# First four pairs of a two-by-two block product: eight products a group, or seven a group with the two groups in turn

## The chip, the cores and the metric

The kernel runs on one core of one Trainium2 chip. The core has a matrix engine (TensorE, PE in the tables; the loading of its stationary operand is PEld), a vector engine (VectorE, DVE), a scalar engine (ScalarE, ACT), a general engine (GpSimd, POOL) and a queue that mostly starts transfers (SyncE, SP). Each engine takes its instructions strictly in the order written for it, and waits where an operand is not ready or a buffer is not free. The metric is device time of one execution in microseconds; lower is better. A difference of 0.2% is about what a measurement of this kernel can tell.

## The reference

`x` is 64 batches of 64 x 1024 numbers. Cut to what matters:

```python
W = weights[condition]                    # per batch a 64 x 64 matrix, one of 16
c = einsum('bct,bcd->bdt', x, W)          # mixes the 64 rows of a batch
logits = c @ gate_w.T + expert_bias       # 4 experts
top1 = argmax(logits)
base = c @ W_up.T                         # 1024 x 1024
z = c @ lora_A.T                          # 4 experts x rank 8
out = x + base + (z of the top expert) @ lora_B of that expert
```

The kernel uses that the mixing of rows and the product over columns can be exchanged: it first forms `u = x @ w` with `w` = gate, lora_A and W_up side by side (1024 x 1060), and then mixes the rows of `u` by a block-diagonal matrix of two batches.

## The kernel before

**Tiling.** A *pair* is two batches: 128 rows of 1024 numbers. There are 32 pairs, and a *group* `g` is the pairs `a = 2g` and `b = 2g + 1`. The product of a group is a two-by-two block product. On the left A11 and A12 are the two column halves of pair a, A21 and A22 those of pair b (each 128 x 512, loaded transposed by `load_half`, L102). On the right B11, B12, B21, B22 are the quarters of `w`, 512 x 530 each: the first index is the half of the 1024 rows, the second the half of the 1060 columns. A block of `w` is handled in four slices k of 128 rows.

**Precision.** Each operand is kept as a high part (rounded to the format in which the matrix engine multiplies) and a low part (the remainder). ACT writes the high part, DVE then subtracts it from the original: `split_a` (L131) for the left, `split_b` (L148) and `split_bs` (L158) for the right. Every product is three matrix products (high-high, high-low, low-high) for each of 4 slices and 2 column banks: 24 matmuls of 264 or 266 columns (`part_of_product`, L198).

**Groups 0 and 1** (`eight`, L505) form all eight block products. In group 0, two products share each of B11 and B21 (a *double* step: for each k first the one pair and then the other); the rest are single. `h` and `at(s, k, ...)` are a table written out by hand: after slice k of step s (k = -1: ahead of the step) the listed work is put into the queues. `run` (L491) and `product` (L214) write out matmuls and hooks in that order, and the wrapper `InOrder` (L35) holds PE, DVE, ACT, POOL and most of SP to it.

**Groups 2 to 15** (`seven`, L622) form seven products each from sums of blocks: S1 to S4 on the left (`sums`, L109) and T1 to T4 on the right. The T blocks are built once, while groups 0 and 1 run: `sum_t1` (L169) subtracts B12 from B11, and `add_to` (L165) starts a transfer on POOL that adds another block of `w` to a tile in place. B11 and B12 are loaded a second time for it (`load_two`, L154). B12 was split for groups 0 and 1 into the memory that T4 takes later.

**After a product** the sums in PSUM become `u` (`u_of` L255, `u_sum` L262: high part by ACT, low part by DVE). For each of three column ranges of a pair, `apply` (L312) mixes the rows, `gate` (L322) picks the expert (six small DVE instructions), `turn` (L341) transposes the result on PE and splits it (ACT, then DVE), `delta` (L349) adds the expert's part, and `evict` (L355) copies to `y` on ACT. After the third range POOL starts a transfer that adds `x` to `y`, and when it has landed SP stores `y`.

PSUM holds three accumulators (`chain`, L195). Work tiles of 530 columns come from a pool of ten (`temp`, L98), halves of `x` from a pool of six, split left operands from a pool of four.

## Time and profile before

| | |
|---|---|
| median of 3 runs | 414.96 us (414.76 to 415.2) |
| the profiled execution: its own time | 415.4 us |
| its span, first to last instruction | 413.6 us |
| busy: PE, DVE, ACT, POOL | 408.5, 285.6, 185.0, 75.0 us |
| granted TensorE clock, mean | 0.999 |
| first matmul of the products | 4.20 us |
| end of the first double step | 12.16 us |
| first matmul of group 2 | about 57.7 us |
| one group of seven afterwards | 24.79 us for two groups (75.40 to 100.19 in the chain) |

The span is 1.8 us shorter than the execution's own time, and that execution is 0.4 us above the median. A busy share is a mean over all stages: DVE has 69% over the span, but 44.64 of the first 57.75 us (77%). The time of a matmul in the groups (about 287 ns) is its own from start to end; in a stream the next starts about 0.124 us after it, since they are pipelined.

### The profile page before, as it was taken

Reading aid. Unit: us, or ns where it says so; the run is one execution under the profiler, and the core shown is the slowest. Engines: PE = TensorE matmul, PEld = TensorE weight load, DVE = VectorE, ACT = ScalarE, POOL = GpSimd, SP = SyncE. Lnnn points to the kernel's source line nnn. Section 1 sums busy time; section 2 is a strip of 40 time slices with the busy share of each in tenths; the row PEclk is TensorE's granted clock in tenths of the full one; section 3 lists DMA queues with packets and bytes.
Section 4 is the critical chain, followed back from the end, with each engine's and each line's share of the span. In section 5 each row is a group of like instructions: output and inputs, shape, how many; then the busy total and the mean of one; then the engine's idle time right before and its main releaser. Section 6 shows DMA issues by size and latency. Waiting matters only on the chain.

```text
span 413.6 us, 8160 instructions
## 1 busy us (share of the span) xinstructions
PE 408.5 (99%) x3191; PEld 407.7 (99%) x3191; DVE 285.6 (69%) x648; ACT 185.0 (45%) x419; POOL 75.0 (18%) x92
## 2 busy tenths in 40 slices
PE   8999999999999999999999999999999999999996
PEld 8999999999999999999999999999999999999995
DVE  5987776876767666676676767666676676766766
ACT  5846734453534445333343534445333344533531
POOL 4304502020020202102020020202102020020000
PEclk9999999999999999999999999999999999999999
DMA  8889964553556435465453555434465443564345
GB/s 276 301 305 224 241 167 98 137 123 99 172 133 177 92 93 143 124 178 135 103 127 98 164 135 159 128 81 138 122 179 135 104 126 94 169 165 124 52 101 178
DMA packets 25830, 60.99 MB, mean 147 GB/s; under 512 B 3328, under 2 KB 5344, under 8 KB 25792
## 3 DMA queue, kind: packets, MB, share of 16 engines
q1 hardware_dynamic: 18112, 40.48, 27.2%
q0 software_dynamic: 6704, 19.21, 27.1%
q10 hardware_dynamic: 976, 0.79, 0.6%
q8 instruction: 25, 0.41, 0.4%
q14 instruction: 13, 0.11, 0.1%
HBM read 43.68 MB, written 16.78 MB: 146 GB/s over the span
## 4 chain that ended last, share of the span: by engine, by line
PE 97%; DMA 1%; issue 0%; POOL 0%; DVE 0%; POOLq 0%
PE c L43 81%; PE o L43 16%; DMA cond_sb<-in_cond_dram 1%; DVE y L43 0%; POOL which L43 0%; POOL condf L43 0%; POOLq L43 0%; POOLq L818 0%
## 5 line engine op out<-in xcount | busy, mean ns | idle before, releaser
L43 PE MATMUL c<-hT,ah 128*128 128x264 f32 x480 | 139.7, 291 | 0.0
L43 PE MATMUL c<-lT,ah 128*128 128x264 f32 x480 | 137.3, 286 | 0.0
L43 PE MATMUL c<-hT,al 128*128 128x264 f32 x480 | 137.1, 286 | 0.0
L43 PE MATMUL c<-hB,ah 128*128 128x264 f32 (+1 forms) x424 | 121.8, 289 | 0.0
L43 PE MATMUL c<-hB,al 128*128 128x264 f32 (+1 forms) x424 | 121.0, 287 | 0.0
L43 PE MATMUL c<-lB,ah 128*128 128x264 f32 (+1 forms) x424 | 119.0, 287 | 0.0
L43 PEld LDWEIGHTS c<-lT,ah 128*128 128x128 f32 x480 | 91.0, 190 | 0.0
L43 PEld LDWEIGHTS c<-hT,ah 128*128 128x128 f32 x480 | 90.9, 189 | 0.0
L43 PEld LDWEIGHTS c<-hT,al 128*128 128x128 f32 x480 | 90.6, 189 | 0.0
L43 POOL DMA_DIRECT2D y<-in_x_dram x31 | 29.3, 945 | 290.3 <-ACT y L43 285.3
L43 PEld LDWEIGHTS c<-hB,ah 128*128 128x128 f32 x424 | 80.7, 190 | 0.3 <-ACT hB L43 0.2
L43 PEld LDWEIGHTS c<-hB,al 128*128 128x128 f32 x424 | 80.7, 190 | 0.0
L43 PEld LDWEIGHTS c<-lB,ah 128*128 128x128 f32 x424 | 79.5, 190 | 0.2 <-issue 0.2
L43 ACT COPY y<-o 128x352 f32<-128x352 f32 (+1 forms) x91 | 40.1, 443 | 58.4 <-PE o L43 55.0
L43 ACT CAST uh<-usum 128x530 fp32r<-128x530 f32 (+4 forms) x44 | 27.1, 616 | 68.4 <-DVE usum L43 68.4
L43 DVE TENSOR_TENSOR al<-S,ah 128x512 fp32r<-128x512 f32 x56 | 38.5, 688 | 24.2 <-ACT ah L43 24.2
L43 DVE TENSOR_TENSOR al<-xh,ah 128x512 fp32r<-128x512 f32 x46 | 31.7, 689 | 30.0 <-ACT ah L43 30.0
L43 PE MATMUL o<-uh,bd 128*128 128x356 f32 (+2 forms) x186 | 44.7, 322 | 0.0
L43 DVE TENSOR_TENSOR ul<-usum,uh 128x530 fp32r<-128x530 f32 (+4 forms) x44 | 30.0, 682 | 18.6 <-ACT uh L43 18.6
L43 ACT CAST zt<-o 96x128 fp32r<-96x128 f32 x31 | 8.1, 262 | 76.0 <-PE o L43 76.0
L43 POOL DMA_INDIRECT wsel<-in_cw_dram,idx x32 | 34.9, 1089 | 10.6 <-issue 5.2
L43 ACT CAST ah<-S 128x512 fp32r<-128x512 f32 x56 | 34.9, 623 | 1.8 <-DVE S L43 1.4
(88 smaller groups left out, 471.3 us busy)
## 6 DMA issues: line engine op xcount, KB each, us to landing
xh<-in_xt_dram SPq DMA_DIRECT2D x60, 256.0 KB
y<-in_x_dram POOLq DMA_DIRECT2D x30, 512.0 KB, 5.6
out_dram<-y SPq DMA_DIRECT2D x30, 512.0 KB
wraw<-in_w_dram SPq DMA_DIRECT2D x23, 265.0 KB
T<-in_w_dram POOLq DMA_DIRECT2D x8, 265.0 KB, 7.3
xx<-in_xt_dram SPq DMA_DIRECT2D x1, 512.0 KB
wsel<-in_cw_dram,idx POOLq DMA_INDIRECT x32, 5.0
y<-in_x_dram SPq DMA_DIRECT2D x1, 512.0 KB
```

Source lines behind the costliest of these rows:

```text
L43: return lambda *a, **k: self.tc.keep_in_program_order(fn(*a, **k))
```

## The change

Groups 0 and 1 are run together by one function, `front`, in place of `eight(0)` and `eight(1)`, with seven products for each: first both groups' A11 by B11 and A12 by B21 as double steps (the first taken pairs are 0 and 2, where they were 0 and 1), then S4 by B22, S1 by T1, S2 by T2, S3 by T3 and A22 by T4, each for group 0 and then for group 1: 14 products instead of 16. B12 is neither loaded nor split. T1 is the plain copy of B11, negated in place, with B12 added by a transfer (two slices in one); T2 is T1 minus B22, computed on DVE; T3 is the negated B22 with B12 added; T4 is T2's tile with B21 added. The plain copies of B11 and B22 stay in memory that the low and high parts of T3 take later. The signs of S1 to S4 and T1 to T4 change accordingly.

In PSUM, `p` holds A11 B11 and then A11 B11 + A12 B21; `q` is S4 B22; `s` collects S1 T1, S2 T2, S3 T3 and A22 T4 one after another. What is needed of a state in between is copied out: A11 B11 alone (`keep_p`, ACT), it plus q (`add_p`, DVE) and it minus S1 T1 (`less_s`, DVE). In the second double step the products of group 0 for k = 0 and 1 are put ahead of those of group 1, with the work listed for k = 0 and k = 1 after each of them.

The diff, cut to its core:

```diff
-    wh["B12"], wl["B12"] = wh["T4"], wl["T4"]
+    before = {
+        q: cpool.tile([P, KH if q != "T2" else 2, NB], F32, name=q, tag=tag)
+        for q, tag in (("B11", "lT3"), ("B22", "hT3"), ("T3", "hT4"), ("T2", "lT4b"))
+    }
...
-        (sync if i < 4 else nc.sync).dma_start(t, xt[i, hf])
+        (sync if i < 6 else nc.sync).dma_start(t, xt[i, hf])
...
+            "S1": (vector.tensor_add, (b, 0), (b, 1)),
+            "S2": (vector.tensor_sub, (a, 0), (g, "S1")),
+            "S3": (vector.tensor_sub, (b, 0), (a, 0)),
+            "S4": (vector.tensor_add, (a, 1), (g, "S2")),
...
+    def start_t1(s):
+        t = before["B11"][:, s]
+        scalar.mul(t, t, -1.0)
+        add_block("T1", s, "B12")
+    def start_t3(s):
+        scalar.mul(before["T3"][:, s], before["B22"][:, s], -1.0)
+        add_block("T3", s, "B12")
+    def end_t1(s):
+        high_t("T1", s)
+        for ks, t in pieces_of("T2", s):
+            vector.tensor_sub(t, before["B11"][:, ks], before["B22"][:, ks])
+        low_t("T1", s)
+    def end_t2(s):
+        high_t("T2", s)
+        low_t("T2", s)
+        add_block("T2", s, "B21")
...
-                raw[i, hf] = t[:, i]
+                raw[2 * i, hf] = t[:, i]
...
+    for i in (1, 3):
+        for hf in range(2):
+            load_half(i, hf)
+    for k in range(KH):
+        load_b("B22", k)
...
+        at(0, 0, split_b, "B21", 0)
+        at(0, 1, split_b, "B21", 1)
+        at(0, 1, split_a, 1, "A12")
+        at(0, 2, split_b, "B21", 2)
+        at(0, 3, split_b, "B21", 3)
+        at(1, -1, load_b3)
+        at(1, -1, keep_p, 0)
+        at(1, -1, keep_p, 1)
+        for m in ("S1", "S2", "S4"):
+            at(1, 0, sums, 0, m)
+        at(1, 0, split_a, 0, "S4")
+        at(1, 1, start_t1, TWOS[0])
+        at(1, 1, split_b, "B22", 0)
+        for m in ("S1", "S2", "S4"):
+            at(1, 1, sums, 1, m)
+        at(1, 2, start_t1, TWOS[1])
+        at(1, 2, split_b, "B22", 1)
+        at(1, 2, split_a, 1, "S4")
+        at(1, 3, split_cond, 0)
+        at(2, -1, lambda: u_of(0, 0, c["p", 0]))
+        at(2, 0, split_b, "B22", 2)
+        at(2, 0, lambda: u_of(2, 0, c["p", 1]))
+        at(2, 1, split_b, "B22", 3)
+        at(2, 2, split_a, 0, "S1")
+        at(2, 3, split_b3, PARTS[0])
+        at(2, 3, apply, 0, 0)
+        at(2, 3, gate, 0)
+        at(3, -1, add_p, 0)
+        at(3, 0, end_t1, TWOS[0])
+        at(3, 1, split_a, 1, "S1")
+        at(3, 2, end_t1, TWOS[1])
+        for s in TWOS:
+            at(3, 3, start_t3, s)
+        at(3, 3, turn, 0)
+        at(3, 3, split_cond, 2)
+        at(4, -1, add_p, 1)
+        at(4, 0, end_t2, TWOS[0])
+        at(4, 1, delta, 0, 0)
+        at(4, 1, evict, 0, 0)
+        at(4, 1, split_b3, PARTS[1])
+        at(4, 1, apply, 2, 0)
+        at(4, 1, gate, 2)
+        at(4, 2, split_a, 0, "S2")
+        at(4, 3, end_t2, TWOS[1])
+        at(5, -1, less_s, 0)
+        at(5, 1, turn, 2)
+        at(5, 1, split_a, 1, "S2")
+        at(5, 2, sums, 0, "S3")
+        at(5, 3, delta, 2, 0)
+        at(5, 3, evict, 2, 0)
+        at(6, -1, less_s, 1)
+        at(6, 0, split_a, 0, "S3")
+        at(6, 1, end_t3, TWOS[0])
+        at(6, 1, sums, 1, "S3")
+        at(6, 2, load_half, 5, 0)
+        at(6, 2, load_half, 5, 1)
+        at(6, 3, end_t3, TWOS[1])
+        at(7, -1, lambda: u_sum(0, 1, c["s", 0], ts["q", 0]))
+        at(7, 0, split_a, 1, "S3")
+        at(7, 2, finish, 0, 1)
+        at(7, 3, finish, 0, 2)
+        at(8, -1, lambda: u_sum(2, 1, c["s", 1], ts["q", 1]))
+        at(8, 0, split_a, 0, "A22")
+        at(8, 1, end_t4, TWOS[0])
+        at(8, 2, finish, 2, 1)
+        at(8, 3, finish, 2, 2)
+        at(8, 3, load_half, 4, 0)
+        at(8, 3, load_half, 4, 1)
+        at(8, 3, split_a, 1, "A22")
+        at(9, -1, lambda: u_sum(1, 1, c["s", 0], ts["p", 0]))
+        at(9, 0, end_t4, TWOS[1])
+        at(9, 1, sums, 2, "S1")
+        at(9, 2, split_cond, 1)
+        at(9, 2, split_cond, 3)
...
+        at(10, -1, lambda: u_sum(3, 1, c["s", 1], ts["p", 1]))
+        at(10, 0, sums, 2, "S2")
+        at(10, 1, split_a, 2, "A11")
+        at(10, 2, sums, 2, "S3")
+        at(11, -1, lambda: u_sum(1, 0, c["s", 0], ts["r", 0]))
+        at(11, 0, split_a, 2, "S2")
+        at(11, 1, sums, 2, "S4")
...
-            at(0, 0, lambda: u_of(pb, 0, cp["1"]))
+            at(0, 0, lambda: u_sum(pb, 0, cp["s", 1], ts["r", 1]))
...
-            for k in range(KH):
-                at(1 + k, 3, split_b, "T4", k)
```

## The prediction

> **What bounds the kernel now.** First the page's busy times and the chain that ended last:

> ```profile
> PE 408.5 (99%) x3191; PEld 407.7 (99%) x3191; DVE 285.6 (69%) x648; ACT 185.0 (45%) x419; POOL 75.0 (18%) x92
> PE c L43 81%; PE o L43 16%; DMA cond_sb<-in_cond_dram 1%; DVE y L43 0%; POOL which L43 0%; POOL condf L43 0%; POOLq L43 0%; POOLq L818 0%
> ```

> PE carries 97% of the chain. The chain in order of time gives the price of a product:

> ```profile
> 7.43 13.04 PE c L43 x102
> 66.45 2.97 PE c L43 x24
> ```

> 24 matmuls take 2.97 us, 0.124 us each. PE waits for nobody after 7.43 us. So a matmul less is worth its time only while the other engines stay ahead. How far ahead are they in the changed stage? Busy time by stretch (columns: length, then PE, PEld, DVE, ACT, POOL, clock, DMA share, GB/s):

> ```profile
> 0.00:12.20 12.20, 11.05 (x81) 10.61 (x82) 6.81 (x21) 7.43 (x17) 6.53 (x23) 1.00 0.86 295
> 0.00:57.75 57.75, 56.60 (x443) 56.16 (x444) 44.64 (x93) 35.72 (x74) 19.82 (x37) 1.00 0.93 268
> 15.00:20.00 5.00, 5.00 (x43) 5.00 (x42) 4.84 (x11) 4.56 (x11) 0.00 (x0) 1.00 0.78 248
> ```

> Group 2 begins at 57.75. Until then DVE works 44.64 us; ahead of 12.2 us it is idle for 12.2 - 6.8 = 5.4 us, waiting for loads, and from 15 to 20 us it is full. Not PE but DVE is short here.

> **Durations**, from the rows in order of time:

> ```profile
> 11.96 1.71 ACT L43 CAST hB<-wraw 128x530 fp32r<-128x530 f32 x3
> 18.19 0.59 ACT L43 CAST uh<-c 128x530 fp32r<-128x530 f32 x1
> 18.68 0.64 ACT L43 CAST hB<-wraw 128x530 fp32r<-128x530 f32 x1
> 12.80 1.94 DVE L43 TENSOR_TENSOR lB<-wraw,hB 128x530 fp32r<-128x530 f32 x3
> 52.44 0.97 DVE L43 TENSOR_TENSOR bd<-wsel,bd 64x64 fp32r<-64x64 f32 x4
> 21.00 0.16 DVE L43 TENSOR_TENSOR lg<-o,bias_sb 128x4 f32<-128x4 f32 x1 [0.71 <-PE o L43]
> 22.40 0.70 DVE L43 TENSOR_TENSOR ul<-c,uh 128x530 fp32r<-128x530 f32 x1
> ```

> From start to start ACT takes 0.54 us for 530 columns, 0.49 from PSUM (18.19 to 18.68). DVE takes 0.62 for 530, 0.60 for 512 (sums and splits follow one another at that step from 54.65 us), 0.25 for a 64 x 64 piece, 1.40 for the six of a gate (21.00 to 22.40). Two slices in one (1060 columns) are not in the trace: no more than two singles (1.24 DVE, 1.08 ACT) and no less than two without the second one's fixed part (264 columns start every 0.35 and 0.32 us, so 1.16 and 0.98). I take 1.16 and 0.98, the rows' slope.

> **What goes and comes, by amount.** PE loses 2 x 24 matmuls: 48 x 0.124 = 5.9 us. The mixing, turning and expert matmuls stay the same in number. On DVE, until group 2: gone are 4 lows of B12, 8 subtractions for T1 and T3 and 12 lows of T1 to T3, 24 x 0.62 = 14.9. In come T1 to T4 as 7 wide and 6 single ones (7 x 1.16 + 6 x 0.62 = 11.9), 8 sums S (4.8), 14 left splits for 8 (3.6), 4 of `add_p` and `less_s` (2.5) and 5 sums ahead of `u` (3.1). Net 25.9 - 14.9 = +11.0. DVE then has 44.6 + 11.0 + 5.4 idle at the start = 61.0 us ahead of group 2, without any other pause. PE's matmuls alone would be there at 57.75 - 5.9 = 51.8. This floor says +3.3 us, and the order of the queues decides what comes on top. Transfers: 12 plain loads of 265 KB less, adding transfers 3.25 MB for 2.1; POOL issues 7 for 8.

> **The queues, step by step** (the program order of the changed kernel, laid on the clock with these durations; the same done to the old program gives no wait of PE and its transpositions at 22.95 and 28.86 us, where the trace has 23.00 and 28.93).

> 1. *Second double step.* `keep_p` must copy A11 B11 out before PE may add to that accumulator. On ACT it stands behind all four B21 casts, the last of which ends at 13.67 (11.96 + 1.71). Copy 0.49 and hand-over 0.1: 14.25. PE is ready at 12.16. **2.1**. The matmuls queued behind all wait.
> 2. *S4 by B22, group 0*, from 14.25 + 5.94 = 20.2. DVE: three sums from 14.75 to 16.6; ACT split 17.2, then on ACT negation of B11 (0.98), B22 slice 0, negation, slice 1. DVE: low of S4 at 17.4, low of slice 0 to 19.5, then three sums of group 1 (21.3), slice 1 (21.95), low of S4 (22.6), two `bd` pieces, a `u` (23.8), slice 2 (24.4), a `u`, slice 3 (25.65). PE waits at slice 1 for 0.9, slice 2 for the cast 0.9 and the low 0.8, slice 3 for 0.5: **3.1**. End 26.3.
> 3. *S1 by T1.* S4 by B22 of group 1, apply and turn take PE to 29.9. DVE goes on: low of S1 26.2, b3 piece, gate after its apply 27.0 to 28.5, `add_p` 29.1, T2 half 30.3, low of T1 31.5. **1.6**. `delta` of pair 0 then waits for a turned z that stands behind split, two T2 slices and T1's second low: 34.75 for 32.9, **1.9**, and 0.2 for `bd`.
> 4. *Step 5*: the gate of pair 2 stands behind `add_p`, T2's low and the larger b3 piece, **0.8** at the turn, and its z behind split, two lows and `less_s`: **1.2**.
> 5. *S2 by T2 of group 1, `finish` of pair 0*: its `u` is summed after two T3 lows and two S3, at 48.4; cast 49.0, low 49.8. PE is there at 47.45: **1.7 and 0.4**.
> 6. *A22 by T4, group 1*: the accumulator is free when `u_sum` of pair 3 has read it, behind two T4 lows, S1 and four `bd` pieces: **1.3**.
> 7. *Into group 2.* The half of pair 4 is on SP in program order behind the stores of pairs 0 and 2, and the second store waits for the transfer that adds x. Rows for that:

> ```profile
> 35.12 0.86 POOL L43 DMA_DIRECT2D y<-in_x_dram  x1 [0.39 <-ACT y L43]
> 66.01 0.86 POOL L43 DMA_DIRECT2D y<-in_x_dram  x1 [13.81 <-ACT y L43]
> 43.63 6.99 SPq L374 DMA_DIRECT2D out_dram<-y  x2
> 71.18 0.34 SPq L374 DMA_DIRECT2D out_dram<-y  x1
> T<-in_w_dram POOLq DMA_DIRECT2D x8, 265.0 KB, 7.3
> ```

> The store follows its addition by 5.2 us in a quiet stage and 8.5 in the crowded front. Eviction ends at 56.5; the adding transfers for T are over by then, so I take 5.5: store 62.0, load 62.5. A load of 256 KB alone is not shown; the first ones (issued at 0.74, used from 3.4) say 2.6, behind a 512 KB store at up to 392 GB/s (the best stretch) 3.9: 65.1 to 66.4, taken 65.9, cast and low to 67.0 where PE is ready at 66.1. **0.9**. While DVE waits for that half in S2, the sum for `u` of pair 1 stands behind it: **1.4 and 0.4** at its apply, **0.3** at the turn, **2.0** at `delta` behind the `u` of pair 3 and a split.

> Sum of waits: 2.1 + 3.1 + 1.6 + 1.9 + 0.2 + 0.8 + 1.2 + 2.1 + 1.3 + 5.0 = 19.3. Less 5.9: +13.4. After that the groups run as before. The profiled execution would span 413.6 + 13.4 = 427.0 (415.4 + 13.4 = 428.8 with what lies around it); it stood 0.4 above the median, which gives 414.96 + 13.4 = **428.4 us**.

> Costed at nothing: T1's transfer, started at 18.3 and 20.1, landing 7.3 to 8.5 later (26.8, 28.6). It is hidden only because DVE comes to T2 at 29.1; with a faster DVE it would be the next to be late. T3 and T2 start at 30 to 41 and are used at 44 to 59.

> [...] The clock row reads 1.00 in every stretch up to 400 us, and 0.96 from 400 to 414 us where PE is busy for only 9.68 of 14. [...]

> **Rivals.**
> - *The cover holds* (faster): PE stays without a wait, 414.96 - 5.9 = 409.0. For it: no wait in 400 us, DVE idle for 31% of the span. Against: the 61.0 us floor. It decides where all waits together are below 5.9. 4%.
> - *Only steps 1 and 2 wait*: 414.96 - 5.9 + 5.2 = 414.3, no difference. It needs DVE to catch up from 26 us on, against the same floor. 3%.
> - *DVE catches up by step 5*, so that 5 to 7 (8.4) vanish: 420.0. For it: ACT and DVE have pauses after 43 us, waiting for each other and for PE. 16%.
> - *More*: additions land after 8.5 us as in the crowded front (3.0 more in step 7), or one clock window: 431.4, both 433. 19%.
> - My sum, 425 to 431 in itself: 58%.
> - That the 48 matmuls do not go is excluded: program order has them gone.

> The range, 419.5 to 432.5, takes in the catch-up and most of the last. Within 0.2% (0.83 us, about what a measurement tells from no change) lies only part of the second rival: 2%; faster 5%, slower 93%.

> **What would show it.** In the profile after: 3143 matmuls; the first long idle of PE at 12.2 us with ACT as releaser; DVE (lB, lT, zt) as releaser between 21 and 42; DVE near full from 13 to 50 us; group 2's first matmul at 66 to 67.5; from about 85 us the same 24.8 us for two groups. I am wrong if PE is past the second double step before 19 us, or if ACT has its copies ahead of the B21 casts.

## The result, and the profile after

The changed kernel takes 431.22 us (median of four, 430.84 to 433.02), the kernel before beside it 415.0 us: 1.0399 times, 95% interval 1.037 to 1.0429. That is slower by 16.2 us; 428.4 was predicted, with a range to 432.5.

First the page's busy times and the chain by engine, profile of the changed kernel:

```profile
PE 409.4 (95%) x3143; PEld 404.8 (94%) x3143; DVE 295.1 (69%) x657; ACT 187.9 (44%) x417; POOL 76.0 (18%) x91
PE 83%; DVE 8%; DMA 5%; ACT 2%; issue 1%; DVEq 0%; ACTq 0%
```

The 48 matmuls are gone (3143 for 3191), but PE carries only 83% of the chain, where it had 97%. The same stretches as before (length, PE, PEld, DVE, ACT, POOL, clock, DMA share, GB/s), and the fullest ones:

```profile
0.00:12.20 12.20, 10.51 (x80) 9.73 (x80) 7.63 (x22) 8.16 (x18) 7.35 (x24) 1.00 0.87 298
0.00:57.75 57.75, 48.21 (x334) 45.46 (x335) 45.79 (x87) 35.87 (x65) 17.82 (x34) 0.94 0.74 177
20.00:30.00 10.00, 8.62 (x63) 7.80 (x61) 9.18 (x20) 7.51 (x13) 0.70 (x1) 1.00 0.78 138
30.00:40.00 10.00, 6.99 (x40) 6.56 (x40) 9.64 (x20) 5.50 (x11) 3.55 (x3) 0.83 0.75 119
```

By 57.75 us PE has done 334 matmuls instead of 443, and DVE is at 92 and 96% from 20 to 40 us. The clock is no longer 1.00 (0.94 up to 57.75 us, 0.83 from 30 to 40). What PE waited for, from its rows in order of time (start, length, what; in brackets the idle time ahead and who ended it):

```profile
13.48 0.39 PE L43 MATMUL c<-hB,ah 128*128 128x264 f32 x1 [1.98 <-ACT t L43]
...
23.41 0.39 PE L43 MATMUL c<-hB,ah 128*128 128x264 f32 x1 [0.76 <-ACT hB L43]
...
31.32 0.39 PE L43 MATMUL c<-lT,ah 128*128 128x264 f32 x1 [1.31 <-DVE lT L43]
...
34.66 0.41 PE L43 MATMUL o<-b,zt 96*128 96x320 f32 x1 [1.70 <-DVE zt L43]
...
49.48 0.58 PE L43 MATMUL o<-uh,bd 128*128 128x352 f32 x2 [1.67 <-ACT uh L43]
...
63.81 0.39 PE L43 MATMUL c<-hT,ah 128*128 128x264 f32 x1 [1.22 <-DVE usum L43]
...
67.76 0.39 PE L43 MATMUL c<-hB,ah 128*128 128x264 f32 x1 [0.72 <-ACT ah L43]
...
70.38 0.60 PE L43 MATMUL o<-uh,bd 128*128 128x356 f32 x2 [1.12 <-ACT uh L43]
...
76.56 0.42 PE L43 MATMUL o<-b,zt 96*128 96x320 f32 x1 [1.87 <-DVE zt L43]
```

These are the places that the prediction named. From 80 to 400 us PE waits for nobody. The last addition to y is then done at 424.70 us, against 410.16 before: +14.5. The span is 15.5 longer; the last us lies behind that addition (4.4 us to the end for 3.4): the last transfer that adds `x` is issued 15.4 us later (419.69 for 404.33), and SP's last stores begin as much later (423.72 for 408.30). Why it is issued late was not looked into. Step 7's load, in the chain in order of time:

```profile
61.53 0.60 DVE S L43
...
62.87 4.20 DMA xh<-in_xt_dram
...
67.09 0.69 DVE S L43
```

One thing the prediction did not have. PE's stretches of 3.4 us (length, PE busy, clock, DMA share, GB/s):

```profile
11.20:14.60 3.40, 1.42 (x12) 1.00 1.06 377
14.60:18.00 3.40, 3.40 (x18) 0.52 1.09 355
...
31.60:35.00 3.40, 1.70 (x13) 1.00 0.77 115
35.00:38.40 3.40, 3.40 (x16) 0.53 1.11 197
```

After 3.4 us in which PE was busy for 1.42 or 1.70, it ran 3.4 us at half clock (0.52 and 0.53): 18 or 16 matmuls in a stretch that holds 27.

### The profile page after: what moved, and what is told of

Read it like the earlier page. It is cut to its first block, busy times and chain, and to the rows that moved or that the text cites. A ratio compares the mean times of both kernels' runs of the same rounds, so it can differ in the third digit from the quotient of the medians.

```text
span 429.1 us, 8033 instructions
## 1 busy us (share of the span) xinstructions
PE 409.4 (95%) x3143; PEld 404.8 (94%) x3143; DVE 295.1 (69%) x657; ACT 187.9 (44%) x417; POOL 76.0 (18%) x91
## 4 chain that ended last, share of the span: by engine, by line
PE 83%; DVE 8%; DMA 5%; ACT 2%; issue 1%; DVEq 0%; ACTq 0%
PE c L43 68%; PE o L43 15%; DMA xh<-in_xt_dram 2%; DMA xx<-in_xt_dram 2%; DVE lT L43 1%; DVE S L43 1%; DVE al L43 1%; DMA b3f<-in_lb_dram 1%; DVE ul L43 1%; ACT uh L43 1%; DVE usum L43 1%; DVE T L43 1%; ACT hT L43 0%; DVE t L43 0%; ACT ah L43 0%
## 5 line engine op out<-in xcount | busy, mean ns | idle before, releaser
L43 PE MATMUL c<-hT,ah 128*128 128x264 f32 (+1 forms) x512 | 149.4, 292 | 1.2 <-DVE usum L43 1.2
L43 PE MATMUL c<-hT,al 128*128 128x264 f32 (+1 forms) x512 | 146.5, 286 | 0.0
L43 PE MATMUL c<-hB,ah 128*128 128x264 f32 x376 | 108.9, 291 | 3.5 <-ACT t L43 2.0
L43 PE MATMUL c<-lT,ah 128*128 128x264 f32 (+1 forms) x384 | 110.1, 287 | 1.3 <-DVE lT L43 1.3
L43 PE MATMUL c<-hB,al 128*128 128x264 f32 x376 | 107.8, 288 | 0.2 <-DVE al L43 0.2
L43 PE MATMUL c<-lB,ah 128*128 128x264 f32 x376 | 106.1, 289 | 0.6 <-DVE lB L43 0.6
L43 PEld LDWEIGHTS c<-hT,ah 128*128 128x128 f32 x512 | 97.2, 190 | 1.4 <-DVE usum L43 1.4
L43 PEld LDWEIGHTS c<-hT,al 128*128 128x128 f32 x512 | 97.2, 190 | 0.0
L43 POOL DMA_DIRECT2D y<-in_x_dram x31 | 28.5, 918 | 309.9 <-ACT y L43 304.1
L43 PEld LDWEIGHTS c<-hB,ah 128*128 128x128 f32 x376 | 72.0, 191 | 4.2 <-ACT t L43 2.2
L43 PEld LDWEIGHTS c<-lT,ah 128*128 128x128 f32 x384 | 73.3, 191 | 1.5 <-DVE lT L43 1.5
L43 PEld LDWEIGHTS c<-lB,ah 128*128 128x128 f32 x376 | 71.1, 192 | 1.4 <-DVE lB L43 1.2
L43 PEld LDWEIGHTS c<-hB,al 128*128 128x128 f32 x376 | 71.8, 191 | 0.4 <-DVE al L43 0.4
L43 ACT COPY y<-o 128x352 f32<-128x352 f32 (+1 forms) x91 | 40.2, 442 | 64.0 <-PE o L43 62.0
L43 ACT CAST uh<-usum 128x530 fp32r<-128x530 f32 (+4 forms) x50 | 30.9, 618 | 80.1 <-DVE usum L43 80.1
L43 DVE TENSOR_TENSOR al<-S,ah 128x512 fp32r<-128x512 f32 x64 | 44.0, 688 | 26.2 <-ACT ah L43 26.1
L43 DVE TENSOR_TENSOR al<-xh,ah 128x512 fp32r<-128x512 f32 x44 | 30.4, 690 | 31.5 <-ACT ah L43 31.5
L43 DVE TENSOR_TENSOR ul<-usum,uh 128x530 fp32r<-128x530 f32 (+4 forms) x50 | 34.3, 685 | 23.1 <-ACT uh L43 23.1
L43 PE MATMUL o<-uh,bd 128*128 128x356 f32 (+2 forms) x186 | 45.7, 326 | 2.8 <-ACT uh L43 2.8
L43 ACT CAST ah<-S 128x512 fp32r<-128x512 f32 x64 | 39.9, 623 | 4.3 <-DVE S L43 3.9
L43 ACT CAST zt<-o 96x128 fp32r<-96x128 f32 x31 | 8.1, 260 | 76.3 <-PE o L43 76.3
L43 POOL DMA_INDIRECT wsel<-in_cw_dram,idx x32 | 35.7, 1114 | 11.4 <-issue 4.9
## 6 DMA issues: line engine op xcount, KB each, us to landing
B<-in_w_dram SPq DMA_DIRECT2D x7, 265.0 KB, 6.0
wraw<-in_w_dram SPq DMA_DIRECT2D x4, 265.0 KB, 6.0
T<-in_w_dram POOLq DMA_DIRECT2D x2, 265.0 KB, 5.1
```

The source lines that it names most:

```text
L43: return lambda *a, **k: self.tc.keep_in_program_order(fn(*a, **k))
```

## The experiments

Two explanations had to be told apart, and a third came with the trace: the order of ACT's and DVE's queues (the prediction), single prices that add up however they stand, and the clock. All kernels start from the changed one. Times in us; "over before" is each median less that of before measured beside it; half clock and PE's idle time (waits over 0.15, from 10 to 80-100 us) are of the profiled execution, which is one of the two (e7) to four behind each median. Beside the different runs before lies between 414.46 and 415.0 us, so two of them are compared by the time over before. The half clock leaves out the first microseconds, ahead of the trace's first entry of the clock (at 4.5 us in the changed kernel; more on this in the last section).

| run | edit | median | over before | half clock | PE idle |
|---|---|---|---|---|---|
| changed kernel | | 431.2 | 16.2 | 6.8 | 13.7 |
| e1 | copies of A11 B11 first | 432.9 | 18.4 | 23.9 | 11.8 |
| e2 | zeros in two waits | 431.6 | 17.1 | 3.4 | 11.9 |
| e3 | halves of pair 4 early | 431.3 | 16.9 | 13.7 | 12.4 |
| e6 | no sums | 429.4 | 14.9 | 17.1 | 10.7 |
| e7 | sums on POOL | 439.2 | 24.3 | 23.9 | 15.5 |
| e8 | zeros in all waits, in accumulators in use | 434.1 | 19.2 | 0 | 6.1 |
| e10 | zeros in all waits | 430.4 | 15.9 | 0 | 4.3 |
| e9 | e10, six more subtractions | 434.8 | 20.3 | 0 | 5.6 |
| e11 | e10, halves of pair 4 early | 428.5 | 13.8 | 0 | 3.1 |
| e12 | e10, no sums | 428.9 | 14.2 | 3.4 | 4.7 |
| e13 | another order | 422.3 | 7.6 | 0 | 8.4 |
| e14 | e13, no sums | 422.1 | 7.5 | 3.4 | 7.3 |

(In e8 to e12 PE's idle time is low because it works on zeros.)

**e1: step 1 by itself.**

```
-        at(0, 2, split_b, "B21", 2)
-        at(0, 3, split_b, "B21", 3)
...
         at(1, -1, keep_p, 1)
+        at(1, -1, split_b, "B21", 2)
+        at(1, -1, split_b, "B21", 3)
```

> The casts and lows of B21 slices 2 and 3 go behind the two copies of A11 B11; nothing else changes. My theory (the order of ACT's and DVE's queues bounds the front): PE's first long wait, 1.98 us ending at 13.48, falls to 1.1 to 1.3 us, but the two slices' work is only moved: S4 and the B22 slices come later by as much, PE waits 3 to 4 us between 18 and 26 us where it waited 2.0, and the end moves by -1 to +1 us against the changed kernel's 431.2. The half-clock stretch from 14.6 to 18.0 us should go, since the wait ahead of it is shorter; its 1.5 us then turn up as waits at B22. Rival (each wait is a price of its own): 0.8 us less for the wait and 1.5 us less for the clock, 428.9 us.

The wait fell from 1.98 to 1.08 us and the half-clock stretch behind it went. But PE then waited 2.8 us between 18.9 and 25 us (3 to 4 were expected), 1.52 of it in one piece ahead of a low of B22, and later periods ran at half clock instead: 23.9 us in the profiled execution (434.62 us, clock 0.971), less in the others (432.46 at 0.987). The rival that each wait is a price of its own is out; the end even went the wrong way, by 2.2 us over before (1.7 by the medians).

**e2: zeros in two waits.**

```
         at(1, -1, keep_p, 1)
+        at(1, -1, keep_warm, 36)
...
+        at(4, 1, warm_in, 32)
         at(4, 1, delta, 0, 0)
```

> Adds 36 matmuls of 128 columns on zeros to PE's queue ahead of the second double step and 32 ahead of the delta of pair 0; PE does them while it would wait (11.3 to 13.5 and 33 to 34.7 us). If the idle time of PE is what halves the clock, PE's clock stays at 1.00 from 14 to 18 and from 35 to 38.5 us. My theory: the 1.5 us that each half-clock stretch cost come back as waits for DVE at the first B22 slice (0.9) and at the turn of pair 2 (0.8), so the end moves by 0 to -1.5 us: 429.7 to 431.2. Rival (the clock is a price of its own): -3.0 us, 428.2. Third: the clock halves all the same, which would say that another cause than PE's idle time stands behind it.

The second group of matmuls on zeros is written, as an accumulation of its own, into 128 columns of the accumulator in which S1 T1 is being added up, so this kernel does not keep that product whole. Both half-clock stretches went (the clock reads 1.00 from 14 to 18 and from 35 to 38 us, with PE busy throughout, where it had read 0.52 and 0.53), so it was PE's idle time that had halved the clock there. What they had hidden came back: 2.62 us of waits around B22 (1.38 in the changed kernel), 0.76 at the turn of pair 2 (none) and 0.93 at its delta (0.36). A new stretch, 26.6 to 30.0 (0.53), followed the waits around B22 (PE busy for 1.96 of the 3.4 us ahead of it). The end did not come earlier: 431.6, and 0.9 more over before. With the new stretch in it this run doesn't settle what the clock costs; e10 does.

**e3: the halves of pair 4 early.**

```
         at(6, 2, load_half, 5, 1)
+        at(6, 2, load_half, 4, 0)
...
         at(8, 0, split_a, 0, "A22")
+        at(8, 1, load_half, 4, 1)
...
-        at(8, 3, load_half, 4, 0)
-        at(8, 3, load_half, 4, 1)
```

> The halves of pair 4 are issued on SP ahead of the stores of pairs 0 and 2, not behind them. My theory (the load stands in SP's queue behind a store that waits for its addition): S of group 2 is ready when DVE comes to it, the wait of PE before the sum of u of pair 1 (1.22 at 63.81) and those for A11's high and low (0.72, 0.21) shrink, group 2's first matmul comes 1.0 to 1.6 us before 67.76 and the end with it: 429.6 to 430.2 us. Rival (DVE's order holds group 2 back anyway, since the sums of u stand behind T4's lows): below 0.3 us of change.

The waits for A11's high and low went, as expected, but nothing was gained: 13.7 us at half clock in the profiled execution where the changed kernel had 6.8. Its edit begins at step 6, and yet its clock already differs at 14.6 us (none) and 24.0 us (a stretch). Whether a period falls so that it is half idle differs from one execution to another; a comparison over 1 us needs the clock held.

**e6: less work on DVE.**

```
-        for m in ("S1", "S2", "S4"):
-            at(1, 0, sums, 0, m)
+        raw[0, "S1"], raw[0, "S2"], raw[0, "S4"] = raw[1, 0], raw[1, 1], raw[1, 0]
+        raw[1, "S1"], raw[1, "S2"], raw[1, "S4"] = raw[3, 0], raw[3, 1], raw[3, 0]
...
-        for m in ("S1", "S2", "S4"):
-            at(1, 1, sums, 1, m)
```

> Leaves out part of the computation: the six sums S1, S2, S4 of groups 0 and 1 are not formed (raw halves of the odd pair are used in their place), all else is as in the changed kernel. DVE has 6 x 0.60 = 3.6 us less to do between 14 and 22 us. My theory (DVE's amount of work bounds PE from 18 to 36 us): PE reaches the turn of pair 0 2.3 to 3.6 us earlier and the end is 2.3 to 3.0 us below 431.2: 428.2 to 428.9. The waits at S1 T1 and behind it stay as they are. Rival (the transfers of T1 or the casts of ACT hold PE back there): below 1 us of gain, and the wait turns up at lT1 or hB22 instead.

First turn at 26.70 us for 29.61, the waits behind it still there (1.73 for 1.31 at S1 T1, 1.73 for 1.70 at delta). The median is 1.9 below the changed kernel's, 1.3 by the time over before, not 2.3 to 3.0, with 17.1 us at half clock.

**e7: the sums on POOL.**

```
+        e = pool if g < 2 else vector
         f, one, two = {
-            "S1": (vector.tensor_add, (b, 0), (b, 1)),
+            "S1": (e.tensor_add, (b, 0), (b, 1)),
...
```

> The sums S1 to S4 of groups 0 and 1 are formed by POOL instead of DVE, in the same program order. DVE has 8 x 0.60 = 4.8 us less to do. My theory: PE waits for the last link of a queue, not for a total: on POOL the sums of group 1 stand in the way of T1's transfers, and the copy to S4 of group 1 on ACT stands ahead of the casts of B22; if a sum takes POOL 1.2 us (not shown so far; from 0.6, as on DVE, to 2.0), the wait for the third slice of B22 becomes about 4 us long and the end lies 2 to 6 us above 431.2. Rival (DVE's total of 61.0 us is the bound): the end is up to 4 us below 431.2. What one sum takes on POOL is measured here in any case.

It came out 8.1 us above the changed kernel (24.3 over before for 16.2), more than I gave it. PE waited 4.6 us around B22 (1.38 in the changed kernel), 2.00 of it in one piece, not about 4. T1's second transfer was issued behind the sums, at 26.22 us for 19.50. Rows of POOL, then of DVE, of this kernel:

```profile
21.07 1.77 POOL L43 TENSOR_TENSOR S<-xh 128x512 f32<-128x512 f32 x1
22.92 3.36 POOL L43 TENSOR_TENSOR S<-xx,S 128x512 f32<-128x512 f32 x2
```

```profile
20.48 4.66 DVE L43 TENSOR_TENSOR lB<-B,hB 128x530 fp32r<-128x530 f32 x2 [0.82 <-ACT hB L43]
```

A sum takes POOL 1.27 us at the least (without DVE beside it) and 1.62 to 1.77 here, and DVE is slower beside it as well: two lows of B22, 0.70 us each elsewhere, took 2.94 and 1.80 us. So these sums gain nothing on POOL. Why both are slower beside each other the rows don't show; 2.94 us is more than one sum and one low together (1.77 + 0.70).

**e8 and e10: the clock held.** Matmuls of 128 columns on zeros wherever PE waited, in e10:

```
         at(1, -1, keep_p, 1)
+        at(1, -1, keep_warm, 36)
...
+        at(2, 0, keep_warm, 12)
         at(2, 0, split_b, "B22", 2)
...
+        at(4, -1, warm_in, ("s", 0), 20)
         at(4, -1, add_p, 1)
...
```

> The changed kernel with matmuls of 128 columns on zeros put into PE's queue at each place where PE waited in its trace (36 ahead of the second double step, 44 around the slices of B22, 24 ahead of S1 T1, 32 and 18 ahead of the deltas of pairs 0 and 2, 12 ahead of the turn of pair 2, 28 ahead of the rest of pair 0, 20 ahead of A22 T4, 16 and 32 in group 2), each amount a little below the wait. They go into columns of PSUM that nothing reads, so the result is that of the changed kernel. PE should then show a clock of 1.00 in the whole front, where the four profiles so far (the changed kernel's, the first double step freed, the halves of pair 4 early, no sums) had 6.8, 23.9, 13.7 and 17.1 us at half clock. My theory: what is left is the order of ACT's and DVE's queues alone, 13.4 us above before as in the sum of waits: 427 to 429 us, and all executions within 0.3% of one another. Rival 1 (the time at half clock is taken up by the waits for DVE behind it): 430.5 to 431.5. Rival 2 (the clock is most of the loss): below 425.

In e8 the matmuls on zeros went into the accumulator that is being copied out, and waited for that copy themselves: the first wait ended at 14.48 instead of 13.48. It says only that the clock can be held (1.000 over the execution).

> As the run before with the clock held, but the 36 matmuls ahead of the second double step and those around B22 go into a bank that nobody reads (there they waited for the copies themselves and ended 1.0 us late), the ones of group 2 into the second chain, and the amounts are cut by a tenth; none ahead of A22 T4. The result is that of the changed kernel. The clock should stay at 1.00. My theory (the order of ACT's and DVE's queues): first turn at 29.6 to 30.3 us, first turn of pair 4 at 94 to 95.5, 427 to 430 us. Rival 1 (time at half clock is taken up by the waits behind it): the same 431 as with 6.8 us at half clock. Rival 2 (the clock is most of the loss): below 425.

Clock 1.00 throughout the front. The turns of pair 0 and pair 4:

```profile
29.91 0.27 PE L43 MATMUL o<-ident,z 128*96 128x128 f32 x1
...
95.46 0.27 PE L43 MATMUL o<-ident,z 128*96 128x128 f32 x1
```

The changed kernel has pair 4 at 95.41: in the profiled execution the half clock had cost nothing by then. Over all executions 15.9 over before, against 16.2. The number is rival 1's, just above my 430: what the half clock took, the waits behind it would have taken. So the loss of the changed kernel is not the clock; it is the waits for ACT's and DVE's queues. (How much of them is the order is what e13 asks.) The clock is not free everywhere, though: with the edits that shorten waits it ate the gain, 16.9 for 13.8 with the halves of pair 4 early (e3, e11).

**e9, e11, e12: one cause each, with the clock held.**

```
+        def again(n):
+            t = temp("again")
+            for _ in range(n):
+                vector.tensor_sub(t, ts["p", 1], ts["p", 1])
...
+        at(2, 1, again, 6)
         at(2, 2, split_a, 0, "S1")
```

> As the kernel with the clock held (e10), with six more subtractions of 530 columns on DVE (their result is not used) after the second slice of B22 in program order, where DVE's row of the changed kernel has 9.18 of 10 us busy, and matmuls on zeros for the longer waits ahead of the turn of pair 0 and of S1 T1 (34 and 16 more), so that the clock stays out of it. The result is that of the changed kernel. My theory (DVE is the limit from 13 to 45 us): 6 x 0.62 = 3.7 us more on DVE, of which 3.0 to 3.7 reach the end: 3.0 to 3.7 us above e10. Rival (PE waits for ACT and the transfers; DVE only happens to be the last by little): below 1.5 us.

From the rows of DVE:

```profile
25.15 4.44 DVE L43 TENSOR_TENSOR again<-t 128x530 f32<-128x530 f32 x6
29.51 0.68 DVE L43 TENSOR_TENSOR al<-S,ah 128x512 fp32r<-128x512 f32 x1
```

The six take 4.36 us to the next start: 0.73 each, not 0.62. All six write one tile; whether that is why was not tried. The end moved by 4.4 in the medians, and the turn of pair 4 by 3.7 in the profiled executions (99.13 for 95.46). In this order DVE is the limit from 25 us on, nearly one for one.

> As the kernel with the clock held (e10, 430.4 us), with the halves of pair 4 issued on SP ahead of the stores of pairs 0 and 2. The run with this edit alone (e3) had 13.7 us at half clock where the changed kernel had 6.8 and gained nothing; here the clock is out of it. My theory (step 7: the load stands behind a store that waits for its addition): 0.9 to 1.6 us below e10, the waits for A11's high and low of group 2 (0.41 and 0.22) gone. Rival (group 2 is held back by the sums of u on DVE in any case): within 0.3 us of e10.

The edit is that of e3. The halves of pair 4 are issued at 58.74 and before, not at 63.80 as in e10. 2.1 us below e10 (first turn of group 2 at 71.98 for 73.63): step 7's mechanism holds, and it is worth more than the 0.9 us that I gave it (at the first turn of group 2, 1.7).

> As the kernel with the clock held (e10), and again without the six sums S1, S2, S4 of groups 0 and 1 (part of the computation is left out: raw halves of the odd pair take their place), the matmuls on zeros around B22 cut from 36 to 4 and 8 more ahead of S1 T1. My theory (DVE is the limit from 13 to 45 us): 3.6 us less of DVE work, of which 2.3 to 3.6 us reach the end: 426.8 to 428.1. The run with this edit alone (e6) gained 1.9 with 17.1 us at half clock. Rival (ACT and the transfers are as late): below 1 us of gain.

The edit is that of e6. First turn 2.4 us earlier (27.50), as expected. In the profiled execution only 0.4 of it was left at the first turn of group 2 (73.20 for 73.63): PE waited 0.78 us for A11's high there (0.41 in e10), and a half-clock stretch followed at 68.9. The median kept 1.7, less than the 2.3 expected.

**e13: the same work in another order.** The 155 entries of the front's list (casts and lows apart) were put in an order that leaves PE fewer and shorter waits. Its core:

```
+        at(0, 3, keep_p, 0)
+        at(0, 3, neg_t1, TWOS[0])
+        at(0, 3, keep_p, 1)
+        at(1, -1, hi_b, "B21", 2)
...
+        at(1, 1, lo_b, "B21", 2)
...
+        at(1, 1, load_half, 4, 0)
...
+        at(4, 1, low_t, "T1", TWOS[1])
+        at(5, 2, add_p, 0)
...
+        at(8, 2, finish, 0, 1)
+        at(9, 2, finish, 0, 2)
```

> The changed kernel, every instruction kept and the result the same, with the order of the front's ACT, DVE, SP and POOL work taken anew: casts and lows as entries of their own, the copies of A11 B11 ahead of the third cast of B21, the lows of A12 and B21 behind the first sums, T1's second half, the gates and b3 pieces later, finish of pairs 0 and 2 one to two products later, halves of pair 4 earlier. My theory (the order of the queues costs about 10 us on top of DVE's floor of 3.3): waits of PE of 8 to 10 us in the front where the changed kernel has 13.7 to 20, none above 1.6 us, so little half clock: 420 to 424 us, still above before. Rival 1 (DVE's work alone is the bound): above 428. Rival 2 (the order is all of it): below 417.

422.31 us, 1.0181 times before (1.0164 to 1.0198): 8.6 us below the changed kernel, each against the before measured beside it, with every instruction kept. PE's idle time is 8.4, no wait above 1.45, and from 9.9 us, where its matmuls begin to start 0.12 us apart, the clock reads 1.00 up to 102 us (0.999 over the execution). Still slower than before, though, so it is no version to keep. Its stretches:

```profile
12.00:20.00 8.00, 6.32 (x49) 5.90 (x48) 7.27 (x12) 7.26 (x14) 2.88 (x3) 1.00 1.07 322
20.00:30.00 10.00, 8.57 (x67) 8.10 (x65) 9.70 (x19) 9.20 (x15) 2.14 (x2) 1.00 0.86 178
30.00:40.00 10.00, 7.46 (x54) 6.81 (x54) 9.65 (x22) 5.26 (x11) 2.39 (x2) 1.00 0.30 48
```

**e14: is what is left DVE's amount?** The six sums are taken out of e13 as in e6.

> As the other order (e13, 422.3 us), without the six sums S1, S2, S4 of groups 0 and 1 (part of the computation is left out: raw halves of the odd pair take their place): 3.6 us less of DVE work. Theory 1 (what is left of the loss, 7.6 us, is DVE's amount of work): 2.3 to 3.6 us below e13, 418.7 to 420. Theory 2 (single links hold PE: the lows of B21, the piece of bd, the gate of pair 0 behind ACT's casts, T1's second half): within 0.7 us of e13, the waits ahead of the turn of pair 0 and of S1 T1 stay, since what stands ahead of them is not the sums. The first would say that no order of the same work comes near before; the second that an order has still something to give.

422.14, no difference. The same stretch as the first one above:

```profile
12.00:20.00 8.00, 6.93 (x55) 6.50 (x54) 4.67 (x8) 7.35 (x14) 2.99 (x3) 1.00 1.07 315
```

DVE was free for another 2.6 us there, and PE still came to the turn of pair 0 at 30.55 (30.78 in e13), where it waited 1.96 us for the gate's z. ACT had 91% from 12 to 30 us in e13 and still 87% here. So up to the first turn it is not DVE's amount that holds e13; from 30 to 60 us, where DVE has 90% or more in both, that was not tried.

## Why the prediction was right, point by point

Measured is the time lost from start to start: the start after the wait, less that of the matmul before it, less its 0.124 us.

| step of the prediction | predicted | measured |
|---|---|---|
| 1 second double step behind the B21 casts | 2.1 | 2.1 |
| 2 S4 by B22 | 3.1 | 2.0 |
| 3 S1 by T1, delta, bd | 1.6, 1.9, 0.2 | 1.6, 1.9, 0 |
| 4 turn and delta of pair 2 | 0.8, 1.2 | 0, 0.5 |
| 5 finish of pair 0 | 1.7, 0.4 | 1.8, 0.4 |
| 6 A22 by T4 | 1.3 | 1.4 |
| 7 into group 2 | 0.9, 1.8, 0.3, 2.0 | 1.3, 1.7, 0, 2.0 |
| sum of waits | 19.3 | 16.7 |
| half clock | 0 | 3.0 (6.8 us; a matmul starts every 0.22 us, so 1 - 0.124/0.22 = 0.44 of each is lost) |
| 48 matmuls | -5.9 | -5.9 |
| at the last addition | 13.4 | 13.8 of the measured 14.5 |

Two things stand in no line of it. PE was through the first double step at 11.35 us, not at 12.16 (-0.8), since its matmuls start 0.22 us apart up to 6.6 us in the profile of before, and 0.124 apart from 4.5 us on in this one; that is no effect of the change. And the matmul behind the first one after a wait starts 0.23 us after it (13.48 to 13.71), not 0.124, about 0.1 us for each of 14 waits (+1.4, an estimate). With both the sum is 14.4.

- **The place and the cause of nearly every wait** were right: an engine's program order, read off the list and laid on the clock with one row's durations. e10, with the clock at 1.00, turns pair 0 at 29.91 us; the working had 29.9. In step 1 both ends lay 0.8 us earlier than worked out: PE was ready at 11.35, and ACT's copies began at 12.84, not 13.67. That the wait still is 2.1 is luck.
- **Steps 2 and 4** were too large by 1.1 and 1.5 because PE came to them late, after half-clock stretches; e2 gave most of those waits back when it took the stretches away.
- **The clock** was wrong as a statement: I counted it at nothing, and there were two stretches at half clock, 3.4 us each, with no gap of PE longer than 1.98 us. The 3.0 us that they took stand for the 2.6 that are missing in steps 2 and 4. That this did no harm to the sum is no luck: with the clock held the waits come back and the time is the same (e10), since PE's lost time lay ahead of waits for DVE.
- **Step 7** was mis-sized: the load took 4.2 us from its issue at 62.87 to DVE's start, I had 3.4 from 62.5 on. With the store out of its way (e11) 2.1 us come back.
- **The floor of 61.0 us** was argued from DVE's amount of work and is not confirmed as a floor. In the changed order a subtraction more on DVE moves the end by about its own time (e9), but in another order 3.6 us less of it move nothing (e14). The sum did not rest on it. It had DVE busy without a pause from 12.2 us on; measured are 5.33 of 7.00 us from 13 to 20 (it waits for ACT's casts there) and 33.06 of 37.00 from 13 to 50, so "near full from 13 to 50" held from 20 us on only.
- **What else was to be seen**: group 2's first matmul at 67.76 (66 to 67.5 predicted); the groups behind as before (12.38 us a group, 95.41 to 107.79; 12.39 before). Of the 2.8 us between 428.4 and 431.2, 1.1 are ahead of the last addition, 1.0 behind it, and 0.7 is where the two profiled executions stand to their medians.
- **Of the rivals** "the cover holds" and "only steps 1 and 2" fell with the first 30 us. "DVE catches up by step 5" fell too: steps 5 to 7 measured 8.6 for the predicted 8.4. "More" has the nearest number, 431.4 for 431.2 (my own sum had 425 to 431), but not the cause: the store of pair 2 followed its addition by 5.2 us (57.25 to 62.44), not 8.5, and the half-clock stretches, two and not one, are not what the end waited for (e10). Its 431.4 is the late additions alone (428.4 + 3.0). No run shows the price of a clock window that its 433 has on top, about 1.6 us; what the runs showed in its place is 1.5 us of lost starts in each of two stretches, and an end hardly earlier without them (15.9 over before in e10, 16.2 here).

## What to carry to other kernels

Fewer matmuls are worth their time only in a stage where PE is the engine waited for; ahead of such a change lay every queue's program order on the clock and ask what is late next, as a wait removed by itself (e1) only showed the next one. Where PE began to wait here, the clock joined in (6.8 us at half clock in the changed kernel, 3.4 to 23.9 in e1 to e6), by a phase that differed from one execution to another: hold it with matmuls on zeros in a bank that nobody reads (e10, 1.00 throughout the front) before comparing two orders, or an edit that is right looks worthless (e3, 16.9 over before for 16.2, against e11, 13.8 for 15.9). The order of the same instructions was worth 8.6 of 16.2 us here.

## What the runs showed of the hardware that was not expected

- PE busy for 31 to 47% of a period: half clock in the next one, each time;
- 48 to 57%: sometimes;
- 58% and more: never.

At half clock, periods with PE busy for 43 to 87% were followed by another at half clock, those at 98% and more by full clock. The row of the second case, from e3, where the stretch from 34.2 us went on:

```profile
34.20:37.60 3.40, 2.10 (x8) 0.51 1.12 199
37.60:41.00 3.40, 3.40 (x17) 0.50 0.74 120
41.00:44.40 3.40, 3.40 (x29) 0.99 1.05 176
```

No long gap was needed: in the changed kernel one of 1.98 us within a period (11.2 to 14.6, PE busy for 42%) went ahead of the first stretch and one of 1.70 us (31.7 to 35.1, 50%) ahead of the second (the gap of 1.31 us lies in the period before).

**The first microseconds ran at half speed, and the clock's column doesn't say so.** It reads 1.00 there, although the trace's first entry of the clock comes only at 4.5 us in the changed kernel and at 6.6 in before. Up to there matmuls start 0.22 us apart in before (5.92 to 6.14 to 6.37), as in a half-clock stretch, and 0.12 behind it; in the changed kernel 30 matmuls of 128 columns take 3.38 us there (0.11 each), where 36 of them take 2.18 at full clock (12.29 to 14.47 in e2, 0.06 each). In e3, which begins with the same instructions as the changed kernel, the slower starts last to about 7 us (three matmuls in each 0.2 us, four from 7.6 on), in e13 to 9.9. So two executions can differ at their start before any edit has an effect.

**DVE's subtractions were longer beside POOL's sums**: 2.94 and 1.80 us for 0.70 (e7).
